# A gated cross-attention block on one core: exponentials transposed ahead of the next scores, first parts ahead of the rests, a bank taken out of turn, and jobs of other stages dealt anew

## The chip, the cores and the metric

The program runs on one core of a Trainium2 chip. The core has a TensorE (PE) with its own weight-load path (PEld), a VectorE (DVE), a ScalarE (ACT), a GpSimd (POOL) and a SyncE (SP), which only issues DMAs. Each engine works through its own instructions in the order in which they were written, and semaphores make one engine wait for another. The metric is the device time of one execution in microseconds; the kernel before takes 729.53 us, the median of 4 runs (728.73 to 730.4).

## The reference

`x` holds 8 sequences of 256 tokens by 512 numbers, that is 16 tiles of 128 tokens. Four blocks are added to it one after another:

```
x = x + tanh(g_xattn[0]) * conv_mixer(ctx, ctx, layernorm(x), ssm_kernel, D, head_dim 8)
x = x + tanh(g_ffn[0])   * bitlinear_ffn(layernorm(x), w1, w2, w3)          # 512 -> 1408 -> 512
x = x + tanh(g_xattn[1]) * masked_attention(layernorm(x), ctx, mask)        # 256 keys, no projections
x = x + tanh(g_ffn[1])   * one_bit_ffn(layernorm(x), w1, w2, w3)            # 512 -> 2048 -> 512
```

- The mixer multiplies the context with itself inside each of 32 heads (8 by 8 products), convolves each product along 512 places with the head's kernel, and contracts with the query.
- The first feed-forward network rounds activations to 8 bits per row and weights to -1, 0, 1.
- The attention takes softmax(x ctx^T / sqrt(512)) over unmasked keys and reads the context out with it.
- The second network rounds activations to 8 bits per group of 64, and takes the sign of its weights times their mean magnitude.

## The kernel before

All instructions of each engine are in an order written out by hand; a Python line that is called earlier stands earlier in the queue of its engine. Pools give out buffers in turn, and a buffer's next user waits for its last one.

**Stage 1, the mixer** (about 12 to 181 us of the profile), runs over 32 heads `h`. In each turn ACT copies the query and the context twice side by side (`q_twice`, `ctx_twice`, L307), POOL forms the pair products `kv` (L320, L326) and adds the halves of the earlier products (L388), TensorE runs 20 matmul records (L343) into one of three double banks of `ps_y`, ACT copies a few columns (`half_wrap`, L353), and DVE multiplies with the query (`half_products`, L365, L371, L378) and reduces (L393). A half of a head's matmuls may start when DVE has done the products that lay in its bank three halves earlier. Between these, a table of jobs deals out other work by turn and by slot of the turn: `job(h, "dve", f)` puts `f` behind DVE's products of turn `h`, `"act"` ahead of ACT's column copies, `"pool"` near the end and `"late"` at the very end of the turn. Jobs that matter here prepare stage 2: `first_stats` and `first_inverse` (DVE), `first_sqrt` (ACT) take the layernorm numbers of the first four tiles in pairs `g`; `first_by_act` takes those of tiles 4 to 7 on ACT by five instructions (L154 to L158); `front_norm`, `front_max`, `front_int`, `front_turn` normalise, find the row maximum, round and transpose (by DMA) a tile.

**Stage 2, the first network** (181 to 303 us), runs over the 16 tiles `t`. Three `up_block`s make two products each in banks of `ps_mm` (four banks; `pa`, `pb`, L852), ACT takes Silu of one (`sl`, L860), DVE multiplies (`hh`, L861); then the row maximum (L512), the rounding (L1000, L1018), a transposing DMA to `hqT`, and the product `down0` (L869) two turns later. `ps_o` and `ps_mm` lie where stage 1's `ps_y` was, and the first bank of `ps_mm` is given to a tile `passed` that is never used. `ln_finish` (L166 to L181) turns four tiles' variances into reciprocal roots, three DVE and fourteen POOL instructions.

**Stage 3, the attention** (303 to 380 us), again runs over the tiles. TensorE's order in turn `t` is: `scores(t)` (L938, 8 records), `e_transposed(t-1)` (`tre`, L959, 2 records), `x_transposed(t+2)` (`tr`, L927, 4 records), `readout(t-1)` (`po`, L967, 4 records). `masked` (DVE, L946 to L948) adds the mask and takes the maximum; `exponentials` (ACT, L953) follows; the transposed exponentials are copied out of PSUM by ACT to `eT` (L961), and the readout takes `eT`. ACT also normalises tile `t+3` (L195) and converts pieces of the last network's weights: `w1_signs(k)` issues the load of piece `k` into one of three buffers `w1st`, and its `make` takes the sign (L840) and, for the third matrix, also the sum of magnitudes (L842). `SIGNS[t]` says how many pieces are loaded in turn `t`; they are made in the next turn. Pieces 24 to 31 belong to the second matrix, 32 to 47 to the third.

**Stage 4, the last network** (372 to 728 us): a value is split into a first part `hi` and a rest `lo` (L1135, L1140), and each product runs over both with the same weights `w1q` (`up_products`, L1160; `down`, L1345).

The start issues some matmuls that nothing reads (`warm`, L664): 8, then two small ones, then 10.

Of the kernel before, what the change touches and what calls it, by code (L numbers as in the profile page):

```python
# [21 lines left out]
P = 128  # L22
# [20 lines left out]
def flamingo_gated_kernel(  # L43
# [159 lines left out]
    def load_table(func):  # L203

        nc.scalar.activation(junk1, ln_eps, func)
# [339 lines left out]
    def job(h, slot, f, *a):  # L545
        jobs.setdefault((h, slot), []).append((f, a))
# [71 lines left out]
    for k, h in enumerate(steps1):  # L618
        job(max(h - 2, steps1[k - 2] if k > 1 else 0), "late", load_w1a, k)
        job(h, "act2", abs_w1, k)  # L620
        if k % N1 == N1 - 1:
# [3 lines left out]
            job(h + 2, "dve", mean_w1, i)  # L625
    for g, h in enumerate((22, 25)):
        for k in range(2):
            job(h + k, "dve", first_stats, 2 * g + k)
        job(h + 1, "late", first_sqrt, g)
        job(h + 2, "dve", first_inverse, g)  # L630
    for k in range(2):
# [7 lines left out]

    for k, h in enumerate((24, 25, 28, 29)):  # L640
        job(h, "late", first_by_act, GRP + k)

# [18 lines left out]
    def warm(n):  # L661

        for _ in range(n):
            nc.tensor.matmul(pt[:, :P], ident, ident, start=True, stop=True)  # L664
# [6 lines left out]
    )  # L671
    warm(10)

# [135 lines left out]
    assert not jobs  # L809
    load_table(AF.Silu)  # L810

# [5 lines left out]

    ps_mm.tile([P, 512], F32, tag="mm", name="passed")

# [163 lines left out]
    for t in range(NT + 1):  # L983
        new = t + 2 < NT
        if t < NT:
            hh = p2.tile([P, FF0], F32, tag="hh", name="hh")
        if new:
            front_norm(t + 2)
# [7 lines left out]
        if t < NT:  # L996
            up_block(*x0[t], hh, 0)
        if 1 <= t:
            q = p1.tile([P, FF0], I8, tag="i8h", name="i8h")
            nc.scalar.activation(q, h_.pop(t - 1), AF.Copy, scale=sc)  # L1000
# [30 lines left out]
        if t > 2:  # L1031
            hqT, f3 = hq_.pop(t - 2)
            d_[t - 2] = (down0(hqT), f3)
        if t in FINISH:
            ln_finish(*FINISH[t])
# [17 lines left out]
        sums = []  # L1053
        if t == 0:
            clip_by_act(2, 3)
        if t == 3:
# [95 lines left out]
    def up_products(xT, f):  # L1152

        f0 = f * 512
        pa = ps_mm.tile([P, 512], F32, tag="mm", name="pa4")
        pb = ps_mm.tile([P, 512], F32, tag="mm", name="pb4")
        for i, pp in ((0, pa), (1, pb)):
            for c in range(NL):
                for k in range(2):
                    nc.tensor.matmul(  # L1160
                        pp,
                        xT[k][:, c, :],
                        w1q[i][:, c, f0 : f0 + 512],
                        start=(c == 0 and k == 0),
                        stop=(c == NL - 1 and k == 1),
                    )
        sl = px.tile([P, 512], F32, tag="sl", name="sl4")
        nc.scalar.activation(sl, pa, AF.Silu, scale=wmean1[:, 0:1])  # L1168
        return pb, sl
# [7 lines left out]

    SIGNS = [2, 2, 2, 2, 1, 2, 1, 1, 2, 1, 2, 1, 1, 1, 1]
    e_, r_ = {}, {}
    for t in range(NT + 2):  # L1180
        if t >= 2:
            residual(t - 2, *r_.pop(t - 2))
        if t < NT and t not in ps_:
            ps_[t] = scores(xT_.pop(t), keys[t // 2])
        if 1 <= t <= NT:
            e, den = e_.pop(t - 1)
            fac = small.tile([P, 1], F32, tag="fac", name="fac")
            nc.vector.reciprocal(fac, den)
            nc.vector.tensor_scalar(fac, fac, gates3[(t - 1) // 2], None, ALU.mult)
        if t < NT:  # L1190
            s_nmx = masked(ps_.pop(t), negs[t // 2])
        if t == NT:
            xn4, q, back = front(1)
            times(xn4, q, back)
            up_gate(hh[:, 0:512], *up_products(xT, 0))
        if 1 <= t <= NT:
            eT = e_transposed(e)

        if t == NT - 2:
# [7 lines left out]
        if t + 3 < NT:  # L1207
            xn_[t + 3] = normalised3(t + 3)
        for make in signs:
            make()  # L1210
        signs = []
        if t == NT:
# [36 lines left out]
        if t < len(SIGNS):  # L1249
            signs = [w1_signs(made + k) for k in range(SIGNS[t])]  # L1250
            made += SIGNS[t]
# [218 lines left out]
```

## Time and profile before

| what | value |
|---|---|
| median of 4 runs | 729.53 us (728.73 to 730.4) |
| the profiled execution | 730.04 us, of which the span is 728.2 us |
| TensorE busy | 713.8 us, 98% of the span, 3212 records |
| VectorE / ScalarE / GpSimd busy | 601.5 / 373.9 / 258.4 us |
| time on the chain that ended last, by engine | TensorE 87%, DVE 3%, ACT 2%, DMA 2% |
| stage 1 convolution matmuls (L343) | 640 records, 160.7 us |
| stage 4 products (L1160, L1345) | 1536 records of about 390 ns each |

The times are read like this: a TensorE record's start follows the start of the record before it by the time that the array needs, and its printed length is longer, since records overlap. So idle time of TensorE is found by comparing starts, not by adding lengths. "[0.95 <-DVE prod L378]" at the end of a row means that the engine stood idle for 0.95 us before that instruction and what ended it.

### The profile page before, as it was taken

The numbers are of one execution on the slowest core, as the hardware profiler recorded it, in microseconds if no ns is written. First come the engines' busy times: TensorE is split into PE (matmuls) and PEld (weight loads), VectorE is DVE, ScalarE is ACT, GpSimd is POOL, SyncE is SP. The second block draws the span as 40 slices with busy tenths as digits, with TensorE's granted clock in tenths as the row PEclk, the third lists the DMA queues.
The fourth block names the chain that finished last, engine by engine and source line by source line (L and its number), as shares of the span: only waits on it lengthen the run. The fifth ranks groups of instructions, "written<-read, shape, count | busy, mean of one in ns | idle before, by whom it ended". The sixth has DMA issues, their size and how long they took to land.

```text
span 728.2 us, 10153 instructions
## 1 busy us (share of the span) xinstructions
PE 713.8 (98%) x3212; PEld 531.9 (73%) x3212; DVE 601.5 (83%) x1224; ACT 373.9 (51%) x672; POOL 258.4 (35%) x363
## 2 busy tenths in 40 slices
PE   8999999998999999999999999999999999999997
PEld 6777777776554444566678788888888888888885
DVE  5799889998898887687867988988888988777965
ACT  5677787777778776767742322322212332212322
POOL 4888998989884535433300020000200002000000
PEclk9999999999999999999999999999999999999999
DMA  5865676821146567687604544645554544555443
GB/s 196 269 230 158 205 246 214 275 68 29 36 102 150 136 145 182 154 276 210 204 1 97 115 108 103 111 101 107 119 111 86 108 110 98 117 111 94 99 90 86
DMA packets 149970, 99.36 MB, mean 136 GB/s; under 512 B 83806, under 2 KB 127838, under 8 KB 149918
## 3 DMA queue, kind: packets, MB, share of 16 engines
q1 hardware_dynamic: 149608, 98.38, 52.4%
q0 software_dynamic: 256, 0.26, 0.5%
q8 instruction: 25, 0.41, 0.2%
q14 instruction: 27, 0.22, 0.1%
q10 hardware_dynamic: 54, 0.08, 0.1%
HBM read 75.58 MB, written 5.03 MB: 111 GB/s over the span
## 4 chain that ended last, share of the span: by engine, by line
PE 87%; DVE 3%; ACT 2%; DMA 2%; issue 1%; POOL 1%; SPq 0%; DVEq 0%; ACTq 0%
PE y L343 20%; PE po L1345 16%; PE pb L1160 15%; PE pa L1160 15%; PE po L967 4%; PE po L869 4%; PE pa L852 4%; PE pb L852 4%; PE ps L938 3%; DMA hqT<-qh 1%; PE tr_back L418 1%; DMA w1st<-in_L_w2t 1%; DVE am L512 1%; PE tr L410 1%; DMA sT<-d 1%
## 5 line engine op out<-in xcount | busy, mean ns | idle before, releaser
L343 PE MATMUL y<-kv,toep 128*128 128x288 f32 x640 | 160.7, 407 | 1.6 <-DVE rstd L128 0.8
L343 PEld LDWEIGHTS y<-kv,toep 128*128 128x128 f32 x640 | 119.3, 190 | 34.3 <-ACT y L353 2.1
L1168 ACT ACTIVATE sl<-pa,wmean 128x512 f32<-128x512 f32 x64 | 44.0, 688 | 187.6 <-PE pa L1160 187.6
L1160 PE MATMUL pa<-w,hi 128*128 128x512 f32 x256 | 100.6, 393 | 0.0
L1160 PE MATMUL pb<-w,hi 128*128 128x512 f32 x256 | 99.7, 390 | 0.5 <-DVE hh L1172 0.5
L1345 PE MATMUL po<-w,lo 128*128 128x512 f32 x256 | 99.9, 390 | 0.0
L1160 PE MATMUL pa<-w,lo 128*128 128x512 f32 x256 | 99.7, 389 | 0.0
L1345 PE MATMUL po<-w,hi 128*128 128x512 f32 x256 | 99.6, 389 | 0.0
L1160 PE MATMUL pb<-w,lo 128*128 128x512 f32 x256 | 99.6, 389 | 0.0
L175 POOL TENSOR_TENSOR nwt<-rstd 128x4 f32<-128x4 f32 x33 | 6.6, 199 | 240.9 <-DVE rstd L170 239.2
L320 POOL TENSOR_TENSOR kv<-cx 128x1024 f32<-128x1024 f32 x32 | 60.6, 1894 | 22.6 <-ACT cx L307 22.2
L852 PEld LDWEIGHTS <-xqT 128*128 128x128 bf16 x384 | 37.5, 98 | 39.9 <-issue 2.9
L388 POOL TENSOR_TENSOR prod<-prod 128x1024 f32<-128x1024 f32 x28 | 66.3, 2368 | 0.4 <-DVE prod L378 0.4
L1135 ACT CAST hi<-v 128x512 fp32r<-128x512 f32 x64 | 39.1, 622 | 48.4 <-DVE v L1335 48.4
L1172 DVE SCALAR_TENSOR_TENSOR hh<-pb,wmean,sl 128x512 f32<-128x512 f32 x64 | 47.7, 745 | 14.2 <-PE pb L1160 14.2
L1160 PEld LDWEIGHTS pb<-w,hi 128*128 128x128 f32 x256 | 48.1, 188 | 10.9 <-DVE hh L1172 1.0
L1345 PEld LDWEIGHTS po<-w,lo 128*128 128x128 f32 x256 | 48.1, 188 | 10.9 <-DVE lo L1140 1.0
L1160 PEld LDWEIGHTS pa<-w,hi 128*128 128x128 f32 x256 | 48.1, 188 | 10.4 <-issue 0.5
L1160 PEld LDWEIGHTS pa<-w,lo 128*128 128x128 f32 x256 | 48.1, 188 | 10.4 <-DVE lo L1140 0.2
L1160 PEld LDWEIGHTS pb<-w,lo 128*128 128x128 f32 x256 | 48.1, 188 | 10.0
L1345 PEld LDWEIGHTS po<-w,hi 128*128 128x128 f32 x256 | 48.1, 188 | 9.9
L365 DVE TENSOR_TENSOR prod<-y,qx 128x512 f32<-128x512 f32 x64 | 43.7, 683 | 9.3 <-ACT y L353 3.9
(160 smaller groups left out, 1345.3 us busy)
## 6 DMA issues: line engine op xcount, KB each, us to landing
sT<-d SPq DMA_DIRECT2D x64, 256.0 KB
toep<-ssm_skip SPq DMA_DIRECT2D x31, 256.0 KB
ch<-in_ctx_heads SPq DMA_DIRECT2D x32, 128.0 KB
w1a<-in_L_w1t SPq DMA_DIRECT2D x8, 512.0 KB
w1a<-in_L_w2t SPq DMA_DIRECT2D x8, 512.0 KB
w1st<-in_L_w1t SPq DMA_DIRECT2D x16, 256.0 KB
w1st<-in_L_w2t SPq DMA_DIRECT2D x16, 256.0 KB
cT<-in_ctx_t SPq DMA_DIRECT2D x8, 512.0 KB
```

The costliest lines, as they stand in the source:

```text
L320: nc.gpsimd.tensor_tensor(kv[:, :, 0 : ND * HD].rearrange("p a (i d) -> p a i d", d=ND), cx[:, :, 0:HD].unsqueeze(3).to_broadcast([P, NL * ...
L343: nc.tensor.matmul(y[:, k, :, W0 : W0 + NPAIR], toeps[h][:, d * P : (d + 1) * P], kvs[h][:, mi * B : (mi + 1) * B, :].rearrange("p b n -> ...
L365: nc.vector.tensor_tensor(prod[:, 0, r, :, :], yv[:, :, W0 : W0 + ND * HD].rearrange("p a (i d) -> p a i d", d=ND), view(q, [HX, n], [1, H ...
L388: nc.gpsimd.tensor_tensor(flat[0], flat[0], flat[1], ALU.add)
L852: nc.tensor.matmul(pp[:, :fw], xqT[:, c, :], w0q[i][:, c, f0 : f0 + fw], start=(c == 0), stop=(c == NL - 1),)
L869: nc.tensor.matmul(po, hqT[:, c, :], w0q[2][:, c, :], start=(c == 0), stop=(c == NF0 - 1))
L967: nc.tensor.matmul(po, eT[:, c, :], cN[:, c, :], start=(c == 0), stop=(c == S // P - 1))
L1135: nc.scalar.copy(hi, v)
L1160: nc.tensor.matmul(pp, xT[k][:, c, :], w1q[i][:, c, f0 : f0 + 512], start=(c == 0 and k == 0), stop=(c == NL - 1 and k == 1),)
L1168: nc.scalar.activation(sl, pa, AF.Silu, scale=wmean1[:, 0:1])
L1172: nc.vector.scalar_tensor_tensor(hh, pb, wmean1[:, 1:2], sl, op0=ALU.mult, op1=ALU.mult)
L1345: nc.tensor.matmul(po, hT[b][k][:, c, :], w1q[2][:, b * NL + c, :], start=(b == 0 and c == 0 and k == 0), stop=(b == NB - 1 and c == NL - ...
```

## The change

- In stage 1, `first_stats`, `first_sqrt` and `first_inverse` move to other turns: pair 0 from turns 22, 23, 23, 24 to 19, 21, 21, 23, pair 1 from 25, 26, 26, 27 to 23, 24, 24, 28. The last two `first_by_act` move from the ends of turns 28 and 29 into the `"act"` slot of turns 29 and 30.
- The second run of `warm` has 4 matmuls and not 10.
- The load of the Silu table is now brought about by an instruction that writes a column of `passed`, the first bank of `ps_mm`. With that, the first `pa` of stage 2 waits for the products of half-head (30, 1), the second `pa` for those of (31, 0), and the second `pb` for this instruction; before, the first `pa` waited for those of (31, 0).
- In stage 2's first turn, `front_norm(2)` (ACT) comes behind the first `up_block` and `ln_finish` (DVE, POOL) behind the third.
- In stage 3, turns 1 to 15 transpose the exponentials of the tile before (PE) and copy them out (ACT) ahead of `residual`, `scores` and `masked`. No pieces are made in turn 0, and the two left from stage 2 are made in turn 1 together with turn 0's one. `SIGNS` begins 1, 2, 2, 2, 2, 2 and not 2, 2, 2, 2, 1, 2.
- In stage 4's `up_products`, the loop over first part and rest is now outside that over the four column blocks: four matmuls with `hi`, then four with `lo`.

```diff
-    for g, h in enumerate((22, 25)):
-        for k in range(2):
-            job(h + k, "dve", first_stats, 2 * g + k)
-        job(h + 1, "late", first_sqrt, g)
-        job(h + 2, "dve", first_inverse, g)
+    for g, (h0, h1, h2) in enumerate(((19, 21, 23), (23, 24, 28))):
+        job(h0, "dve", first_stats, 2 * g)
+        job(h1, "dve", first_stats, 2 * g + 1)
+        job(h1, "late", first_sqrt, g)
+        job(h2, "dve", first_inverse, g)
...
-    for k, h in enumerate((24, 25, 28, 29)):
-        job(h, "late", first_by_act, GRP + k)
+    for k, at in enumerate(((24, "late"), (25, "late"), (29, "act"), (30, "act"))):
+        job(*at, first_by_act, GRP + k)
...
-    warm(10)
+    warm(4)
...
-    load_table(AF.Silu)
...
-    ps_mm.tile([P, 512], F32, tag="mm", name="passed")
+    passed = ps_mm.tile([P, 512], F32, tag="mm", name="passed")
+    nc.scalar.activation(passed[:, :1], ln_eps, AF.Silu)
...
-        if new:
+        if new and t > 0:
             front_norm(t + 2)
...
             up_block(*x0[t], hh, 0)
+        if t == 0:
+            front_norm(t + 2)
...
-        if t in FINISH:
+        if t in FINISH and t > 0:
             ln_finish(*FINISH[t])
...
         if t == 0:
+            ln_finish(*FINISH[t])
             clip_by_act(2, 3)
...
         for i, pp in ((0, pa), (1, pb)):
-            for c in range(NL):
-                for k in range(2):
+            for k in range(2):
+                for c in range(NL):
                     nc.tensor.matmul(
...
-    SIGNS = [2, 2, 2, 2, 1, 2, 1, 1, 2, 1, 2, 1, 1, 1, 1]
+    SIGNS = [1, 2, 2, 2, 2, 2, 1, 1, 2, 1, 2, 1, 1, 1, 1]
     e_, r_ = {}, {}
     for t in range(NT + 2):
+        if 1 <= t <= NT:
+            e, den = e_.pop(t - 1)
+        if 1 <= t < NT:
+            eT = e_transposed(e)
         if t >= 2:
             residual(t - 2, *r_.pop(t - 2))
         if t < NT and t not in ps_:
             ps_[t] = scores(xT_.pop(t), keys[t // 2])
         if 1 <= t <= NT:
-            e, den = e_.pop(t - 1)
             fac = small.tile([P, 1], F32, tag="fac", name="fac")
...
-        if 1 <= t <= NT:
+        if t == NT:
             eT = e_transposed(e)
-
...
-        for make in signs:
-            make()
-        signs = []
+        if t > 0:
+            for make in signs:
+                make()
+            signs = []
...
         if t < len(SIGNS):
-            signs = [w1_signs(made + k) for k in range(SIGNS[t])]
+            signs += [w1_signs(made + k) for k in range(SIGNS[t])]
             made += SIGNS[t]
```

## The prediction

> **What bounds the kernel now.** I read three views in this order: busy times and chain, the timeline of an attention turn, the waits. The profile page first:
>
> ```profile
> PE 713.8 (98%) x3212; PEld 531.9 (73%) x3212; DVE 601.5 (83%) x1224; ACT 373.9 (51%) x672; POOL 258.4 (35%) x363
> PE 87%; DVE 3%; ACT 2%; DMA 2%; issue 1%; POOL 1%; SPq 0%; DVEq 0%; ACTq 0%
> ```
>
> TensorE is busy 98% of the span and carries 87% of the chain that ended last. The change removes only six warm-up matmuls, at the start; so elsewhere it can gain only what TensorE loses between starts. I compared each TensorE start with the one before and the usual spacing of that kind, and added up what was over: about 4.9 us in the first 20 us, 4.6 in 140 to 193 (the end of the mixer and the first turn of the network), 1.0 at 292.7, 6.5 in the attention, 0.9 at 401.5 to 402.5, and in 420 to 700 only 0.06 per 20 us. The last network, over 40% of the time, is full.
>
> An attention turn, by the timeline of 326 to 340 us (start, length, engine, line; the last number in brackets is idle time and what ended it):
>
> ```profile
> 330.27 0.38 PE L959 MATMUL tre<-ident,s 128*128 128x128 f32 x2
> 330.49 0.60 PE L927 MATMUL tr<-ident,xn 128*128 128x128 f32 x4
> 330.69 0.37 ACT L961 COPY eT<-tre 128x256 f32<-128x256 f32 x1 [1.37 <-PE tre L959]
> 331.11 0.30 PEld L967 LDWEIGHTS po<-cN,eT 128*128 128x128 f32 x2 [0.26 <-ACT eT L961]
> 331.11 1.98 PE L967 MATMUL po<-cN,eT 128*128 128x512 f32 x4
> 331.13 0.51 ACT L953 ACTIVATE s<-s,nmx 128x256 f32<-128x256 f32 x1
> 332.34 0.61 ACT L840 ACTIVATE w<-w1st 128x512 fp32r<-128x512 f32 x1
> 332.93 1.89 PE L938 MATMUL ps<-cT,xT 128*128 128x256 f32 x8
> ...
> 334.80 0.19 ACT L842 ACTIVATION_READ_ACCUMULATOR w1st<-w1st 128x1 f32 x1
> 334.86 0.42 DVE L946 CUSTOM_DVE_ANT_0 s<-ps,neg 128x256 f32<-128x256 f32 x1 [0.66 <-PE ps L938]
> 335.08 0.37 ACT L961 COPY eT<-tre 128x256 f32<-128x256 f32 x1
> ```
>
> See that a turn of TensorE is 4.39 us (tre 330.27 to 334.66), and that the four `tr` records (0.44) are all that covers the copy `eT`; the readout comes 0.19 after its place, and its first weights are not ahead: 1.82 from the readout's start to the next scores, where a readout without the wait takes 1.71 (367.35 to 369.06). So a turn loses 0.19 + 0.105 = 0.29. See also that ACT, from 331.13 to 334.99, makes an exponential, a normalisation and two pieces of weights that each need a sign and a magnitude sum.
>
> **The change, part by part.** The base is the profiled execution, 730.04 us (span 728.2 and 1.8 around it), 0.5 above the median of 729.53.
>
> *Attention order, gain.* With `tre` ahead of the scores, copy and `eT` have the eight score records (1.73) and `tr` (0.44) as cover, against 0.37 of copy. The turns of tiles 4 to 12 have nine waits of 0.29: -2.65. Tile 3 has 0.35: -0.35. The second readout of the stage waits 1.42 at 311.91, because `eT` stands on ACT behind two signs that wait for loads:
>
> ```profile
> 311.95 0.74 DVE L222 SCALAR_TENSOR_TENSOR xs<-po,fac,xs 128x512 f32<-128x512 f32 x1
> 312.50 0.63 ACT L840 ACTIVATE w<-w1st 128x512 fp32r<-128x512 f32 x1 [1.62 <-DMA w1st<-in_L_w2t]
> 313.03 0.35 ACT L961 COPY eT<-tre 128x256 f32<-128x256 f32 x1
> 313.44 1.12 PE L967 MATMUL po<-cN,eT 128*128 128x512 f32 x2 [1.26 <-ACT eT L961]
> ```
>
> The new order puts `eT` ahead of the signs, and these start a turn later. The readout then starts at about 312.0 and not 313.5, but the next `tre` now follows directly and has its own chain: masked scores at 312.92 (DVE's own order holds them there), exponentials at 313.63 to 314.14; TensorE would be free at 313.74. So 1.5 - 0.45, and with that turn's 0.35 the stage is about 1.4 earlier by tile 2. Together -4.4.
>
> *Attention order, price.* `tre(t)` now needs the exponentials before the next scores. From the end of the scores to the masked ones is 0.20, to the exponentials 0.86, to their end 1.37 plus issue; behind them lie `tr` and readout, 2.15. About 0.7 is left, so TensorE does not wait, if ACT comes at once. But `eT` and the exponentials now have ACT's longest turns between them: ACT needs 0.70 for the exponentials and their sum, 0.71 to the next free place for `xn`, 2.63 from 332.34 to the end of the second magnitude sum at 334.99, and 0.37 for `eT`: 4.41 in all, more than a turn of 4.10. Where `eT` must come 3.68 after the exponentials' start less 0.27 of copy and semaphore, it comes 0.73 late, and 0.17 more in a turn directly behind such a one (its exponentials shift too). By `SIGNS`, pieces from 32 on carry magnitude sums; the turns with two of them are tiles 5, 6, 9 and 11, and tile 4 has one (0.1). 0.73 x 3 + 0.17 + 0.1 = 2.46. I take it whole; it is 0 if the loss is hidden by DVE or by a load that comes later anyway, and it doubles if the late `tre` makes the scores' masks late too, on DVE (83% busy). The number of pieces and loads is 22 before and after; SP's queue has the loads behind those of `cT` and `cN` as before, a turn later for the first pieces, of which ACT has three in turn 1. The waits of ACT for `w1st` are 5.2 us in four places; the first two of these (1.47 and 1.62) move behind `eT`. Sum of the attention: **-1.9**, bounds -4.4 and +0.5.
>
> *End of the mixer.* `first_stats(3)` and `first_sqrt(1)` come earlier: ACT's wait of 1.31 at 161.72 goes, by which column copies and so TensorE were late at 159.66 (0.56). In place of it ACT waits at turn 24 for DVE's statistics (about 150.8 against ACT free at 149.9), 0.95; behind that instruction stand `first_by_act`, the copies of query and context, then POOL's pairs. By hand, the pairs of turn 28 come 1 us later (161.4 against 160.45), and by turn 30 TensorE is 0.4 earlier (the two late `first_by_act` are only moved, 1.7 of ACT each). At the passage into the network:
>
> ```profile
> 178.63 1.86 PE L343 MATMUL y<-kv,toep 128*128 128x288 f32 x7
> 181.45 1.02 PE L852 MATMUL pa<-w,xqT 128*128 128x512 bf16 x4 [0.95 <-DVE prod L378]
> ```
>
> This 0.95 goes, since the first product now takes a bank that was free earlier. But who comes next? ACT loads the Silu table (1.28 from 181.18) and normalises (0.80 from 182.58) before the first Silu at 183.29; moved behind, the normalisation frees 0.7, and the first `hh` would be at 183.4 to 183.7 against 183.99. The banks after that are released at the pace of DVE and ACT. `ln_finish` moves too: its DVE part once took 1.40 beside a POOL instruction (others 0.17), and moved to the turn's end it delays the maximum `am`, for which I get 189.1 against 188.98. So TensorE waits later what it waited at 181.45. I take **-0.2** for both, with bounds -1.8 (what a whole passage would be worth) and +0.9 (turn 24's wait, kept to the end).
>
> *Start.* Six `warm` matmuls less. They run at 0.11 each up to 8 us; the first transposes wait for `xnp` (ACT, 7.80, first weights at 8.01), the next for POOL (10.93). So **0**: the cover is that chain. What they might be worth is that the clock is up. The profile shows a granted clock of 1.00 throughout; but starts are 0.21 apart from 1.46 to 5.2 us and 0.11 from 5.79 on. The 1.62 of idle time before 10.93 did not bring the longer spacing back. [...]
>
> *Last network.* Both orders have the same 1536 records, weights and moving data. The rest `lo` is in time: the only such row is the 0.24 of the weights at 371.73, and it lies under the last readout matmul (four by 0.43 from 369.90 or later). Spacing is 0.2266 with either kind. **0**, bounds -0.8 (two such starts of 0.41 over spacing, 371.32 and 380.83, taken as true) and +1.
>
> Sum: 730.04 - 1.9 - 0.2 = 727.9 in such an execution, less 0.5: **727.4 us** for the median.
>
> **The rivals.** *Whole gain*: ACT catches up within slack, the magnitude turns cost nothing: -4.4, and -0.8 at the passage: 724.3. For it: ACT is only 51% busy, and one turn's lag may be taken by slack of the next. Against: 4.41 in a turn of 4.10 is arithmetic.
>
> *Hidden anyway*: readouts are no longer late, but three pieces in turn 1, their loads and the longer ACT turns return nearly all: -0.5, so 729.0. For it: "ACT w L840" waits 5.2 us for loads and DMA queues are busy (0.79 in 303 to 318). Against: the nine regular waits have no load in them.
>
> *Clock lost, slower*: with six warm matmuls fewer the array is back at the longer spacing when the transposes begin. Work of 8.1 to 17.0 us is
>
> ```profile
> 8.10:17.00 8.90, 7.11 (x46) 5.46 (x45) 7.00 (x23) 6.53 (x13) 4.03 (x4) 1.00 0.50 166
> ```
>
> that is 7.11 us of TensorE, which at twice the spacing is 7.1 more, less 1.8 of idle cover at 9.0 to 10.9: +5.3. With my -2.1 it is +3.2, or 732.7. It decides if it costs more than 3.6 us. Against: six matmuls are a short pause beside the 1.62 that did no harm.
>
> **How the numbers follow.** Forecast 0.50, whole gain 0.22, hidden 0.20, clock lost 0.08. A measurement can tell 0.2%, 1.46 us: faster is below 728.07, slower above 730.99. Forecast: between its bounds mostly faster, 0.34 faster, 0.12 same, 0.04 slower. Whole gain: 0.22 faster. Hidden: 0.07 faster, 0.11 same, 0.02 slower. Clock: 0.02 same, 0.06 slower. Sum 0.63, 0.25, 0.12. The range goes from -6 (the attention whole with a passage at nearly its bound: 723.8) to +1.1 (730.6; both upper bounds, 0.5 and 0.9, less what is unlikely to meet). The forecast's own range is 725.9 to 729.0.
>
> **What would show it.** Right: no idle time before `po` L967 in tiles 3 to 5, a turn of 4.10 there, and about 0.7 before `po` in tiles 5, 6, 9 and 11 ended by `eT`; `masked` waits as before. The first `pa` starts near 180.5, with new idle time before the following products. Starts 0.11 apart at 8 to 17 us; spacing in the last network unchanged. Wrong: turns of 4.10 throughout (whole gain); 0.21 between transposes at 8 us (clock); waits for `w1st` or exponentials of 1 us or more in the attention (hidden); pairs in stage 1 more than 1 us late after turn 28.

## The result and the profile after

The changed kernel takes 731.08 us, the median of 53 executions, against 730.04 us for the kernel before (78 executions on the same chips): 1.0019 times the time, 95% interval 1.0012 to 1.0025, so 0.9 to 1.8 us longer. The forecast was 727.4. The fastest quarter of its executions ends at 730.04 (before: 729.01), the slowest quarter begins at 732.40 (before: 730.87): it is later throughout, and most at the slow end. Its profiled execution took 730.46 us with a span of 728.4, 0.2 more than before's.

The page of the changed kernel, busy engines and the chain that ended last:

```profile
PE 711.2 (98%) x3200; PEld 529.9 (73%) x3200; DVE 600.2 (82%) x1224; ACT 372.5 (51%) x672; POOL 258.3 (35%) x363
PE 77%; POOL 6%; DVE 4%; ACT 4%; issue 4%; DMA 2%; SPq 0%; DVEq 0%; POOLq 0%; ACTq 0%
```

The six matmuls that are gone are 12 records (3212 to 3200). TensorE's part of the chain fell from 87% to 77%, and POOL's rose from 1% to 6%: from about 112 to 160 us the chain now runs largely through POOL's pair products and additions. The timeline of the changed kernel in the mixer, TensorE's turns 21 to 24 (start, length, engine, line; in brackets the idle time before and what ended it):

```profile
125.42 0.62 ACT L307 COPY cx<-ch 128x512 f32<-128x512 f32 x1 [1.42 <-DMA ch<-in_ctx_heads]
...
134.10 0.68 DVE L118 BATCH_NORM_STATS2 st<-xs 128x6 f32<-128x512 f32 x1
134.82 0.18 DVE L119 BATCH_NORM_AGGREGATE mv<-st 128x2 f32<-128x6 f32 x1
134.92 0.66 DVE L365 TENSOR_TENSOR prod<-y,qx 128x512 f32<-128x512 f32 x1
135.03 0.29 ACT L123 ACTIVATE std<-mv,ln_eps 128x2 f32<-128x2 f32 x1 [0.94 <-DVE mv L119]
135.24 0.60 ACT L307 COPY qx<-qT 128x512 f32<-128x512 f32 x1
135.74 0.61 ACT L307 COPY cx<-ch 128x512 f32<-128x512 f32 x1
...
136.18 2.27 DVE L395 TENSOR_REDUCE qT<-prod 128x256 f32<-128x2048 f32 x1
...
136.44 1.89 POOL L320 TENSOR_TENSOR kv<-cx 128x1024 f32<-128x1024 f32 x1 [0.75 <-ACT cx L307]
...
138.58 0.69 DVE L365 TENSOR_TENSOR prod<-y,qx 128x512 f32<-128x512 f32 x1
...
140.10 2.18 PE L343 MATMUL y<-kv,toep 128*128 128x288 f32 x8 [0.66 <-DVE prod L378]
```

and the same products of the kernel before:

```profile
133.11 0.67 DVE L365 TENSOR_TENSOR prod<-y,qx 128x512 f32<-128x512 f32 x1
...
134.40 2.27 DVE L395 TENSOR_REDUCE qT<-prod 128x256 f32<-128x2048 f32 x1
...
136.80 0.69 DVE L365 TENSOR_TENSOR prod<-y,qx 128x512 f32<-128x512 f32 x1
```

At 140.10 TensorE waits for a bank that DVE's products release (those from 138.58 on; before, from 136.80 on), and from 130.80 to there DVE has no idle time. So the products are late by what stands ahead of them on DVE. About 0.9 us of the lateness came in at 125.42, where ACT's copy waits 1.42 us for a load (0.55 in the profile of the kernel before, but 1.27 to 1.65 in ten of the eleven others with the old turns). The rest is `first_stats` of the second tile (L118, L119, 0.86 us), which now precedes the products of 134.92. The profile of e17, a kernel below that has the old turns and the same 1.42, separates the two: its turn 24 takes 5.43 us, that of the changed kernel 6.19, that of the kernel before 5.29. So 0.76 belongs to the statistics. The square root of the first pair, now at the end of turn 21, waits 0.94 us for them on ACT, with the copies of query and context behind it; that wait is not what held DVE here.

The second square root (151.92, a wait of 1.06 us for DVE) does hold the copies behind it, and POOL stands idle for 3.65 us until it makes the next pairs at 155.25. Turn 25 begins 1.00 us later than before, turn 29 2.09; turn 31 is 1.13 late. At the passage:

```profile
181.46 1.03 PE L852 MATMUL pa<-w,xqT 128*128 128x512 bf16 x4
182.27 0.31 ACT L353 COPY y<-y 128x192 f32<-128x192 f32 x1
...
184.00 0.67 ACT L860 ACTIVATE sl<-pa,f 128x512 f32<-128x512 f32 x1
...
188.60 1.26 DVE L166 TENSOR_SCALAR nwv<-mv 128x4 f32<-128x4 f32 x1
...
190.47 1.60 DVE L512 TENSOR_REDUCE am<-hh 128x1 f32<-128x1408 f32 x1
...
193.21 0.81 PE L852 MATMUL pb<-w,xqT 128*128 128x384 bf16 x4 [1.91 <-DVE hh L861]
```

The first `pa` has no wait any more. But counted from the start of turn 31 (176.61), the row maximum `am` comes at 13.86 us (before 13.50) and this last `pb` at 16.60 (before 16.25). What were two waits for the kernel before (0.95 and 0.63) is one wait of 1.91.

In the attention the new order does what it should in most turns. The rows around the exception:

```profile
330.61 0.61 ACT L840 ACTIVATE w<-w1st 128x512 fp32r<-128x512 f32 x1
331.25 0.63 ACT L842 ACTIVATE w1st<-w1st 128x512 f32<-128x512 f32 x1
331.88 0.35 ACT L961 COPY eT<-tre 128x256 f32<-128x256 f32 x1
332.22 0.51 ACT L953 ACTIVATE s<-s,nmx 128x256 f32<-128x256 f32 x1
...
332.29 1.98 PE L967 MATMUL po<-cN,eT 128*128 128x512 f32 x4 [0.32 <-ACT eT L961]
...
336.49 1.88 PE L967 MATMUL po<-cN,eT 128*128 128x512 f32 x4
```

Where ACT has made two pieces with magnitude sums, `eT` is late (332.29, and again at 349.28 and 358.07: 0.48 late and 0.10 for the weights each time); the readout at 336.49 waits for nothing, and turns without the wait are 4.10 us.

### The profile page after: what moved, and what is told of

It reads as the page before. It is cut to its first block, busy times and chain, and to the rows that moved or that the text cites. A ratio compares the mean times of both kernels' runs of the same rounds, so it can differ in the third digit from the quotient of the medians.

```text
span 728.4 us, 10125 instructions
## 1 busy us (share of the span) xinstructions
PE 711.2 (98%) x3200; PEld 529.9 (73%) x3200; DVE 600.2 (82%) x1224; ACT 372.5 (51%) x672; POOL 258.3 (35%) x363
## 4 chain that ended last, share of the span: by engine, by line
PE 77%; POOL 6%; DVE 4%; ACT 4%; issue 4%; DMA 2%; SPq 0%; DVEq 0%; POOLq 0%; ACTq 0%
PE po L1354 16%; PE pb L1164 15%; PE pa L1164 15%; PE y L343 13%; PE po L869 4%; PE pa L852 4%; PE pb L852 4%; PE po L967 3%; POOL prod L388 2%; PE ps L938 2%; POOL kv L320 1%; DMA hqT<-qh 1%; DMA w1st<-in_L_w2t 1%; POOL w L477 1%; ACT w L840 1%
## 5 line engine op out<-in xcount | busy, mean ns | idle before, releaser
L1164 PE MATMUL pa<-w,hi 128*128 128x512 f32 x256 | 69.5, 393 | 0.0
L1164 PE MATMUL pb<-w,hi 128*128 128x512 f32 x256 | 68.6, 390 | 0.4 <-DVE hh L1176 0.4
L1164 PE MATMUL pa<-w,lo 128*128 128x512 f32 x256 | 68.5, 389 | 0.0
L1164 PE MATMUL pb<-w,lo 128*128 128x512 f32 x256 | 68.4, 389 | 0.0
L1164 PEld LDWEIGHTS pb<-w,hi 128*128 128x128 f32 x256 | 48.0, 188 | 10.8 <-DVE hh L1176 0.8
```

Source lines behind the costliest of these rows:

```text
L1164: nc.tensor.matmul(pp, xT[k][:, c, :], w1q[i][:, c, f0 : f0 + 512], start=(c == 0 and k == 0), stop=(c == NL - 1 and k == 1),)
```

## The experiments

Each kernel has 12 executions (e15 and e16: 11) against 23 to 35 of the kernel before on the same chip. "Low" counts the executions whose mean granted TensorE clock is below 0.9985; the kernel before has 37 such among 163 in these comparisons (23%), with a median of 731.8 us against 730.6 for its others, the changed kernel 21 among 54, with 732.5 against 730.2.

| kernel | median us | before us | ratio, 95% interval | low |
|---|---|---|---|---|
| e1 loop order undone | 733.00 | 730.85 | 1.0030, 1.0012 to 1.0048 | 9 |
| e2 attention alone | 730.06 | 730.85 | 0.9993, 0.9979 to 1.0007 | 5 |
| e3 mixer's end and passage alone | 732.71 | 730.85 | 1.0029, 1.0015 to 1.0043 | 6 |
| e4 loop order alone | 731.08 | 730.85 | 1.0003, 0.9993 to 1.0014 | 4 |
| e5 statistics' turns alone | 731.01 | 730.74 | 1.0007, 0.9997 to 1.0018 | 2 |
| e6 two first_by_act alone | 730.41 | 730.74 | 1.0004, 0.9993 to 1.0014 | 3 |
| e7 bank passed alone | 730.09 | 730.74 | 0.9992, 0.9979 to 1.0004 | 3 |
| e8 network's first turn alone | 730.81 | 730.74 | 1.0006, 0.9994 to 1.0017 | 4 |
| e9 changed, warm(10) | 731.88 | 730.76 | 1.0011, 0.9999 to 1.0023 | 6 |
| e10 before, warm(4) | 730.83 | 730.76 | 1.0008, 0.9993 to 1.0024 | 3 |
| e11 changed, start filled | 732.71 | 730.76 | 1.0017, 1.0005 to 1.0030 | 8 |
| e12 before, start filled | 731.10 | 730.76 | 0.9998, 0.9984 to 1.0013 | 0 |
| e13 attention and passed | 730.14 | 730.85 | 0.9991, 0.9981 to 1.0001 | 3 |
| e14 changed, start filled in the transpose's bank | 731.14 | 730.85 | 1.0004, 0.9994 to 1.0015 | 3 |
| e15 as e14, passage filled | 732.23 | 730.85 | 1.0019, 1.0007 to 1.0030 | 4 |
| e16 attention, old SIGNS | 730.99 | 730.85 | 0.9999, 0.9988 to 1.0011 | 4 |
| e17 e13, start filled | 729.69 | 730.94 | 0.9989, 0.9976 to 1.0001 | 0 |
| e18 changed, old jobs | 732.55 | 730.94 | 1.0013, 0.9995 to 1.0030 | 8 |

Most single effects are near what 12 executions can tell. So the profiles are read by segments as well, between starts of TensorE: from turn 1 to turn 31 of the mixer; from there to the attention's first `tre`, without the one wait for `hqT` near 295 us (it is 0.49 to 2.10 over the profiles, with no relation to the kernel); from `tre` to the last scores. Medians over the profiles:

| segment | with the part | without it | difference |
|---|---|---|---|
| mixer, by the statistics' new turns | 157.4 (8 profiles, 157.03 to 157.75) | 156.7 (12, 156.44 to 156.98) | +0.65 |
| to the attention, by the passage's parts together | 127.5 (6, 127.45 to 127.79) | 127.3 (12, 127.14 to 127.56) | +0.2 |
| attention, by the new order with new SIGNS | 60.2 (10, 59.45 to 61.68) | 60.9 (9, 60.62 to 61.85) | -0.7 |
| from the last scores to the end, by the loop order | 362.5 | 362.5 | 0 |

(e15 and e18 are left out of the second row: the one has matmuls added there, the other loses its clock there.)

**Four parts of the change, each taken out or put in alone (e1 to e4).** e1 undoes the loop order in the changed kernel, and e4 makes it in the kernel before:

```diff
-            for k in range(2):
-                for c in range(NL):
+            for c in range(NL):
+                for k in range(2):
```

> The changed kernel with one part undone: the last network's products run again over first part and rest inside the loop over the column blocks. Theory A (the loop is worth nothing, since the rest is in time and the records are the same): span within 0.4 us of the changed kernel's 728.4 and a median within 0.5 us of its 731.1. Rival B (the new order, which changes the weights at every record, lets the granted clock fall more often: the changed kernel's executions at a granted clock of 0.993 to 0.998 took 731.1 to 734.4 us, those at 0.999 and 1.000 mostly 729.1 to 730.7): median 1 us lower than the changed kernel's, and few executions below 0.999.

> The kernel before with the last network's loop order alone. Theory A: within 0.4 us of before, spacing of the products unchanged at 0.227 us. Rival B (granted clock): about 1 us slower than before, with more executions below a granted clock of 0.999.

Rival B fell: e1 has more low executions, not fewer, and e4 is no different from the kernel before. Theory A's sizes for e1 were missed: the median (733.0) in an experiment with 9 low executions of 12, the span (729.2) in a profile at the full clock, whose attention has three readouts 0.6 to 0.8 us late behind signs with late loads. The segment behind the attention shows no difference. The loop is worth nothing that these runs resolve.

e2 is the hunk of stage 3 and nothing else (the moved `e_transposed`, `SIGNS`, `t > 0` and `+=`).

> The kernel before with the attention's part alone (transposed exponentials ahead of the scores, and the new SIGNS with no pieces made in turn 0). Theory A (the attention gains what the two traces show between its first transposed exponentials and its last scores, 1.6 us, and the mixer's end and the passage lose it): faster than before by 1.2 to 2.2 us, with the readout late only where two pieces with magnitude sums are made. Rival (the attention gained only because it began 1.95 us later and its loads had landed by then): within 0.6 us of before, with new waits for w1st.

It gained 0.5 us by the ratio, and its interval holds zero: less than Theory A, and within the rival's number, though not for its reason, since no new wait for `w1st` shows. The three late readouts are there, 0.48 each. What is smaller is the gain, and another profile says why. The second readout of e3, which has the old order, by its timeline:

```profile
313.48 0.36 ACT L961 COPY eT<-tre 128x256 f32<-128x256 f32 x1
...
313.89 1.98 PE L967 MATMUL po<-cN,eT 128*128 128x512 f32 x4 [0.18 <-ACT eT L961]
```

This is the readout that waited 1.42 us at 311.91 in the profile on which the forecast was built. In the eight other profiles with the old order it comes 0.19 to 0.34 behind its place: that one execution had a long wait that is not usual (its loads for `w1st` landed at 310.25 and 312.50), and the attention's usual length is 60.9, not 61.85.

e3 is the hunks of stage 1, the Silu table, `front_norm` and `ln_finish`.

> The kernel before with the parts around the mixer's end alone: the new turns of first_stats, first_sqrt, first_inverse and first_by_act, the Silu load by a column of passed, front_norm and ln_finish moved in the first turn of the first network. Theory A: slower than before by 1.3 to 2.2 us; turn 25 begins about 0.9 us late, and the first transposed exponentials of the attention come about 1.9 us late. Rival (it is the loop or the warm-up that costs): within 0.5 us of before.

Theory A held by the ratio, 2.1 us slower (1.1 to 3.1), though half of its executions are low and its profile, with a span 0.6 longer than before's, is not.

**The parts of e3 by themselves (e5 to e8).** e5 is the first hunk of the change (`first_stats`, `first_sqrt`, `first_inverse`), e6 the second (`first_by_act`), e7 `passed` in place of `load_table(AF.Silu)`, e8 `front_norm` and `ln_finish`:

```diff
-    for g, h in enumerate((22, 25)):
...
+    for g, (h0, h1, h2) in enumerate(((19, 21, 23), (23, 24, 28))):
```

> The kernel before with the new turns of first_stats, first_sqrt and first_inverse alone. Theory A (ACT's square root now waits for the statistics at the ends of turns 21 and 24, 0.94 and 1.06 us in the changed kernel, and the copies of query and context stand behind it): turn 25 begins 0.7 to 0.9 us late against turn 24, turn 28 another 0.4; the one old wait of 1.31 us in turn 26 is gone; first product of the network 0.3 to 1 us late, time 0 to +1.2 us. Rival (the waits are covered, what costs lies at the passage): turns as before, time within 0.4 us.

The turns came as late as Theory A said: turn 25 is 1.14 later against turn 24 (a little over the 0.9 expected), turn 28 another 0.46, turn 29 0.64, of which 1.0 is regained by turn 31. The segment of the mixer is 157.75, the longest of all. That the square roots cause all of it is not shown: in turn 24 TensorE waits 0.90 us for DVE's products, as in the changed kernel, and ahead of these stand the statistics themselves. The time, +0.5 us (-0.2 to +1.3), agrees but does not show it alone.

```diff
-    for k, h in enumerate((24, 25, 28, 29)):
-        job(h, "late", first_by_act, GRP + k)
+    for k, at in enumerate(((24, "late"), (25, "late"), (29, "act"), (30, "act"))):
+        job(*at, first_by_act, GRP + k)
```

> The kernel before with the last two first_by_act alone moved, from the ends of turns 28 and 29 ahead of ACT's column copies of turns 29 and 30. Theory A (1.7 us of ACT now stand ahead of the last column copies and of the Silu table): the first Silu and hh of the network come 0.7 to 1.4 us late, the first row maximum with them, time +0.4 to +1.2 us. Rival (ACT has the slack there): first Silu as before at 183.3, time within 0.4 us.

The rival held: the first Silu comes 7.82 us after turn 31 begins, before 7.81.

```diff
-    load_table(AF.Silu)
...
-    ps_mm.tile([P, 512], F32, tag="mm", name="passed")
+    passed = ps_mm.tile([P, 512], F32, tag="mm", name="passed")
+    nc.scalar.activation(passed[:, :1], ln_eps, AF.Silu)
```

> The kernel before with the Silu table loaded by writing a column of the first bank, passed, and nothing else. Theory A (the wait of 0.95 us ahead of the first product only moves behind it, since the first hh is set by ACT and DVE): first product 0.9 us earlier, second row maximum and the attention's start within 0.3 us of before, time within 0.5 us of before. The three kernels with this part had 2.06 to 2.10 us around their spans and the others 1.76 to 1.85; if that belongs to this part, 0.3 us of time is lost outside the span here. Rival (the bank is a real gain): attention's start 0.7 us earlier or more.

Theory A held: counted from turn 31 the first `pa` is 1.1 earlier, a new wait of 0.67 for `hh` follows, and the segment to the attention is 127.14, as before. The 0.3 us around the span are not here (1.78).

```diff
-        if new:
+        if new and t > 0:
             front_norm(t + 2)
...
-        if t in FINISH:
+        if t in FINISH and t > 0:
             ln_finish(*FINISH[t])
```

> The kernel before with front_norm(2) behind the first up_block and ln_finish behind the third in the network's first turn, and nothing else. Theory A (ACT reaches the first Silu 0.7 us sooner, DVE finishes the third hh before the slow statistics instruction of 1.2 to 1.4 us, which then delays the row maximum as before): first hh 0.3 us earlier or more, row maximum of the first hh within 0.3 us of before's 188.98, time within 0.4 us. Rival (the slow instruction and the later normalisation come on top): row maximum 0.7 us late or more, time +0.5 us or more.

Theory A held: from turn 31 the first Silu 7.11 (before 7.81), the first `hh` 8.14 (8.51), `am` 13.54 (13.50).

**The start (e9 to e12).** Two of the first profiles had a mean granted clock below 1: it fell to 0.50 to 0.67 between 12 and 16 us, at an idle stretch of 1.99 us in e5 and 2.79 us in e8, while TensorE waited for POOL's `xnp`. So theory C: what the median shows is lost there. e9 has the changed kernel with `warm(10)`, e10 the kernel before with `warm(4)`; e11 (changed) and e12 (before) add

```diff
     pair_turn(0, 1)
+    fill = [ps_y.tile([P, 2, B, YB], F32, tag="y", name="fill") for _ in range(3)]
+    for _ in range(8):
+        nc.tensor.matmul(
+            fill[0][:, 0, :, W0 : W0 + P // B], ident, ident, start=True, stop=True
+        )
```

> The changed kernel with the second warm-up back at 10 matmuls. Theory C (what the median shows is the granted clock at the start: in two profiles it fell to 0.50 to 0.67 between 12 and 16 us after an idle stretch of 1.99 and 2.79 us, the executions with a mean granted clock below 0.9985 are about 2.2 us longer, and the changed kernel has 21 of 54 of them against 14 of 70 of the kernel before): fewer such executions, about 3 of 12, and a median near 730.3 us. Rival A (the mixer's end costs what the median shows): median unchanged near 731.1.

> The kernel before with the second warm-up cut to 4 matmuls, and nothing else. Theory C: more executions below 0.9985, 5 of 12 or more, and a median 0.5 to 1.5 us above before. Rival (a wait for the first transposes hides the six matmuls and nothing else changes): as before, 2 or 3 of 12, median within 0.4 us.

> The changed kernel with 8 more matmuls that nothing reads between the second and the third of the first transposes, where TensorE stands idle for 1.6 us or longer. Theory C: no execution below 0.9985 or one at most, and a median of 729.6 to 730.4 us, below the changed kernel's. Rival (the clock falls elsewhere, or these executions are long for another reason): the share stays at 4 or 5 of 12 and the median near 731.

> The kernel before with the same 8 matmuls. Theory C: no execution below 0.9985 or one at most, median 0.2 to 0.6 us below before; beside the changed kernel with them it shows what the rest of the change is worth at an undisturbed clock, by the executions so far between -0.5 and +0.3 us. Rival A: the changed kernel with them is 1 us or more slower than this one.

Theory C held for e12 alone: with the stretch filled, none of 12 executions is low, but the median did not fall with it. e9 and e11 kept their low executions, and neither tells where. e9's own profile loses the clock at the start (from 12.27 us, in an idle stretch of 2.67). e11 has another passage than the changed kernel: in its profile the first product of the network waits for the instruction that writes `passed`, where the changed kernel has no wait:

```profile
183.95 1.02 PE L857 MATMUL pa<-w,xqT 128*128 128x512 bf16 x3 [2.50 <-ACT passed L823]
```

In e10 the median is as before, yet three executions have a clock of 0.992 to 0.995, and the mean is 731.5 against 730.9. Its profile shows a third kind of start: records of `warm` and of the transposes stay 0.21 us apart, those of the first products 0.48, until 17.7 us, and turn 1 begins at 22.76 (before 19.04). In the profiles with `warm(10)` the spacing first becomes 0.11 between 4.4 and 6.2 us or between 9.5 and 10.8, and never later.

**The passage (e13 to e16).** The question was where the changed kernel loses its clock: theory D said at the passage, in the wait of 1.91 us. e14 and e15 fill the second idle stretch of the start, into the next transpose's own bank, and e15 adds 16 matmuls ahead of that `pb`; e13 joins e2 and e7; e16 is e2 with the old `SIGNS` and their making in turn 0:

```diff
+    early = ps_tr.tile([P, NL, P], F32, tag="tr", name="tr")
+    for _ in range(8):
+        nc.tensor.matmul(early[:, 0, :], ident, ident, start=True, stop=True)
...
-    pair_turn(1, 1)
+    trs[pairs[1][1]] = early
+    for c in range(NL):
+        nc.tensor.transpose(early[:, c, :], ps_[1][0][1][:, c * P : (c + 1) * P], ident)
...
+            if fill and i == 1:
+                spare = [ps_o.tile([P, L], F32, tag="o", name="po") for _ in range(2)]
+                for _ in range(fill):
+                    nc.tensor.matmul(spare[0][:, :P], ident, ident, start=True, stop=True)
```

> The kernel before with the attention's part and the bank passed, the two parts that were not slower alone. Theory D (these gain 0.3 to 0.8 us each by the executions so far, and leave the passage without a stretch of idle time that costs the clock): faster than before by 0.5 to 1.5 us, 0 or 1 of 12 executions at a granted clock of 0.995 or less. Rival (the gains were noise of the start): within 0.4 us of before.

> The changed kernel with 8 matmuls that nothing reads ahead of the third of the first transposes, written into that transpose's own bank, so that no bank is taken out of turn. Theory D (the changed kernel loses the clock at the passage): still 3 to 7 of 12 executions at 0.995 or less, 2 to 3 us longer than the others; if its profile is one of them, half clock between 191 and 200 us. Rival C (the clock is lost at the start alone): none, median near 730.

> As the kernel before this, with 16 more matmuls that nothing reads in the network's second turn, between the last pa and pb, where TensorE waits 1.9 us for hh. Theory D: 0 or 1 of 12 executions at 0.995 or less, median 729.5 to 730.5 us. Rival: as many low executions as without them.

> The kernel before with the transposed exponentials ahead of the scores, but SIGNS and the making of pieces as before. Theory A (ACT's turns with magnitude sums delay eT by 0.5 to 0.8 us each): readouts late in the turns behind two pieces of the third matrix, those of tiles 8 and 10 at least, and no gain or loss against e2 beyond 0.8 us. Rival (SIGNS is what makes the order pay): 1 us slower than e2, with new waits in the first turns.

e14 and e15 do not bear theory D out: one and two executions at 0.995 or less. e15 is inconclusive besides, since a matmul is two records, and its 16 held TensorE for 3.4 us where 1.9 were to be filled (counted from the first `pa`, that `pb` came 1.5 us later than in the changed kernel). Neither fills the first idle stretch of the start, ahead of the first transposes (0.92 us in e14's profile), so the 7 low executions among their 23 may still come from there. e13 is 0.7 us faster by the ratio, with zero just inside the interval; its one low profile lost the clock from 11.2 to 18.0 us, at the start, in an idle stretch of 2.25. In e16 readouts are 0.48 late near 337, 350 and 359 us, behind magnitude sums, and 0.7 and 0.4 late near 315 and 324; it is 0.4 us above e2, within Theory A's bound, with some of the early waits that the rival named.

**Two last kernels (e17, e18).** e17 is e13 with the start filled as in e14. e18 puts the old two job tables back into the changed kernel, so that e5 and e6 are undone.

> The kernel before with the attention's part, the bank passed and 8 matmuls that nothing reads ahead of the third of the first transposes, in that transpose's own bank; the warm-up stays at 10. By the segments: attention 0.6 us shorter, mixer and network as before, 1.8 us around the span, and fewer executions with a lower granted clock: 0.6 to 1.4 us faster than before. Rival (what the first parts gain is taken back by the start): within 0.4 us of before.

> The changed kernel with the old turns of first_stats, first_sqrt, first_inverse and first_by_act. Theory A (these jobs carry the loss): mixer from turn 1 to turn 31 back to 156.4 to 157.0 us from 157.5, 127.2 us instead of 127.5 from there to the attention without the wait for hqT, median 0.7 to 1.5 us below the changed kernel's and not above before's. Rival (the loss is the start's, with its four warm-up matmuls): median as the changed kernel's, 1 us above before.

e17 is the fastest of all: no low execution, and 0.8 us faster than before (interval -1.8 to +0.1). It beats the changed kernel, whose interval lies wholly above its own; against the kernel before it is likely, not shown. e18 brought the mixer back (156.79) as Theory A said, but not the median: 8 of 12 executions are low, and four others took 729.0 to 731.3. Its profile happens to be the longest of them, at a mean clock of 0.992, and shows where. Windows of e18 (window, its length, PE, PEld, DVE, ACT and POOL busy, granted clock, DMA share, GB/s):

```profile
4.00:8.00 4.00, 2.55 (x18) 2.13 (x17) 2.96 (x11) 1.73 (x4) 2.31 (x2) 0.98 0.98 351
8.00:12.00 4.00, 2.92 (x13) 2.53 (x14) 3.83 (x14) 3.05 (x6) 0.77 (x2) 0.50 0.53 195
12.00:16.00 4.00, 4.00 (x17) 3.21 (x16) 2.00 (x10) 3.00 (x6) 2.54 (x2) 0.66 0.59 197
...
192.00:196.00 4.00, 2.02 (x12) 1.09 (x11) 3.43 (x8) 2.73 (x4) 2.93 (x14) 0.95 0.17 33
196.00:200.00 4.00, 4.00 (x15) 2.02 (x14) 2.99 (x6) 3.07 (x6) 3.73 (x6) 0.62 0.49 92
```

and its timeline at the two places:

```profile
8.05 1.97 PE L410 MATMUL tr<-ident,xnp 128*128 128x128 f32 x8 [1.03 <-ACT xnp L195]
...
193.99 0.81 PE L852 MATMUL pb<-w,xqT 128*128 128x384 bf16 x4 [1.85 <-DVE hh L861]
...
195.37 1.66 PE L852 MATMUL pa<-w,xqT 128*128 128x512 bf16 x4
```

The clock falls first at 7.88 us (a mean of 0.98 over 4 to 8 us), in the idle stretch of 1.03 us that the six warm-up matmuls used to fill; eight transposes take 1.97 us and not 1.19. It falls again behind the 1.85 us wait for `hh`: four `pa` records take 1.66 us where four took 1.03. The segment from turn 31 to the attention is 1.5 us longer than in the other profiles (128.78 against 127.3). In e17's profile, where the spacing becomes 0.11 only at 9.55 us, no fall follows:

```profile
8.00:12.00 4.00, 3.76 (x27) 3.52 (x26) 3.83 (x13) 2.42 (x6) 0.95 (x2) 1.00 0.57 213
12.00:16.00 4.00, 4.00 (x31) 3.63 (x31) 1.70 (x7) 2.81 (x6) 1.18 (x2) 1.00 0.59 197
```

So both places are shown, in one execution. Twelve executions of one kernel cannot tell the shares apart; all of them together tell more. By an estimate, a mean clock of 0.995 over a span of 730 us stands for some 7 us at half the clock; e13's profile, with a mean of 0.995, has 6.8 us of it. The kernel before has 1 such among 163, and the eight kernels with ten warm-up matmuls and without the new mixer's end and passage together (e2, e4 to e8, e13, e16) have 2 among 95. With four warm-up matmuls and an unfilled start there are 26 among 90 (the changed kernel 13 of 54, e1 5, e10 3, e18 5 of 12 each); e10 differs from the kernel before in the warm-up alone (3 of 12 against 1 of 163). So the cut warm-up costs the clock in a share of the executions. With ten warm-up matmuls and the new mixer's end and passage there are 4 among 24 (e3, e9). That is more than without them, but which of their parts does it is open. And the two kernels with ten warm-up matmuls and the second stretch filled (e12, e17) have no low execution among 24, where 5 or 6 would be usual.

## Why the prediction was wrong

**Attention, gain, forecast -4.4: the mechanism was right, a third of the size was not there.** The nine regular waits of 0.29 went. The term of 1.4 for the first two tiles rested on one wait of 1.42 us in one execution; in the eight other profiles of the old order that readout is 0.19 to 0.34 late. The median over executions to which the sum was applied holds no such wait, so it could not be gained. The price of 0.45 that the term was netted against did come: in all ten profiles of the new order with the new `SIGNS`, TensorE waits 0.54 us for the exponentials ahead of the third `tre`.

**Attention, price, forecast 2.46: nearly right.** Three readouts are late by 0.59, 1.77 together; the 0.17 and the 0.1 that were added did not show. In seven of the ten profiles one or more readouts of the first turns are late as well, mostly by 0.2 to 0.8, behind signs whose loads are late. Forecast for the whole -1.9; the segments show about -0.7, and -1.6 against the one profile.

**End of the mixer, forecast -0.2 with the passage: the step that failed.** I followed the second pair's square root on ACT (turn 24; 0.95 forecast, 1.06 measured) and put the earlier statistics of the first pair at nothing. They stand on DVE, which has no idle time there, ahead of products that release TensorE's banks, and cost 0.76 in turn 24. The catching up was overrated too: turn 30, forecast 0.4 early, is 1.54 late. The mixer is 0.65 longer in the segments.

**Passage.** That the wait only moves behind the first product was right, as was `am` (forecast 189.1; 190.47 less the 1.13 of the late turn 31 is 189.3). What I did not cost is that waits of 0.95 and 0.63 are now one of 1.91. The clock fell behind such a wait in e18's profile (1.85), not in the changed kernel's (1.91) or e14's (1.90).

**Start, forecast 0: the second step that failed, wrong in its size and its reasoning.** A warm-up matmul is two records of 0.11 us (six matmuls are 12 records fewer), so the six are 1.3 us of work, not 0.66, and the stretch that they leave open was not costed. I went by one stretch of 1.62 us in one execution, behind which the longer spacing did not come back. The runs show the clock falling in a stretch of 1.03 us (e18), in or just behind five of 1.85 to 2.79 (e5, e8, e9, e13, e16), and not behind five of 1.62 to 1.67 (before, after, e1, e3, e7). No run shows the 0 for executions at large: with the warm-up alone cut (e10), 3 of 12 executions have a clock of 0.995 or less, and 1 of 163 of the kernel before. In the changed kernel's own profile the start cost nothing, which is why only other executions show it. The rival "clock lost" named the place (8 to 17 us) and had a chance of 0.08; it happens in a share of executions. The changed kernel's 13 executions at 0.995 or less have a median of 732.9 us, its 33 at the full clock 730.2.

**Last network, forecast 0:** right, as far as these runs resolve.

**The sum.** By segments: +0.65 mixer, +0.2 to the attention, -0.7 attention, and +0.3 that lies around the span (2.08 us in the changed kernel's executions against 1.77), together about +0.5. For the clock there is an estimate from the executions: 21 low ones of 54, 2.3 us longer than the others, put 0.9 us on the changed kernel's mean, and 37 of 163, 1.2 us longer, put 0.3 on that of the kernel before. The difference of 0.6 and the 0.5 of the segments make 1.1, beside 1.04 between the medians and 1.35 between the means (731.34 against 729.99). How the 0.6 divides between start and passage is open. So is the cause of the 0.3 around the span: none of e5 to e8 has it whole (1.76, 1.89, 1.78, 1.84), nor has e18 (1.87); e3 has (2.07), and so has e17 (2.01), which lacks most of these parts. And 0.5 of the distance between 727.4 and 731.08 lies in the base: four executions of the kernel before had a median of 729.53, 78 have 730.04.

## What to carry to other kernels

A wait that one profile shows is a sample: before a gain is built on it, look for it in the profile of another execution, and count a chance wait for a load as noise. When a job is moved to an earlier turn on an engine that works in order, ask of every one of its instructions whether its input is ready there and what stands behind it. Here a square root of 0.3 us waited 1.06 for its input and held copies and pairs behind it, and 0.86 us of statistics on an engine without idle time held the products behind them for about 0.8. Waits that are gathered into one, and fillers taken out of an idle stretch, have a price that the profiled execution need not show: at two such places TensorE's clock fell to half in e18's profile (idle for 1.03 and 1.85 us) and stayed at 1.00 in the changed kernel's (0.86 and 1.91).

## What the runs showed of the hardware

- The same program starts in several ways. Matmul records of 128 columns go from 0.21 to 0.11 us apart between 4.4 and 6.3 us, between 9.5 and 10.8 us, or (e10) at about 17.7 us. The 20 records of `warm(10)` take 2.50 us in the profiles of the kernel before, e3, e5, e7 and e8, and 4.38 to 4.64 in those of e2, e4 and e6. Turn 1 of the mixer begins at 19.04 us in the profile of the kernel before and at 22.76 in e10's.
- The profile's granted clock reads 1.00 while records are still 0.21 us apart at the start (until 4.4 us at the earliest, in e10 until 17.7). From 12 to 16 us TensorE works on 14 records in 4.00 us of busy time in e10 at a clock of 1.00, 13 in 4.00 in e13 at 0.50, and 22 in 3.83 in the kernel before at 1.00. So the spacing has to be read as well.
- A fall takes the clock to half (windows of 0.50 in e5, e13 and e18). By the means of the windows it lasts 3.40 to 3.44 us (e5, e8, e9, e16, e18 from 195.61) or 6.8 to 6.9 us (e13: 0.90, 0.50 and 0.75 over 8 to 20 us; e18 from 7.88: 0.98, 0.50 and 0.66 over 4 to 16 us).
- The length of an idle stretch does not decide alone: the clock fell in one of 1.03 us (e18) and not behind five of 1.62 to 1.67. Nor does the busy time just before: in the 3.41 us up to its second fall e18's TensorE is busy for 1.49 us, and the clock falls; in the 3.41 us up to 193.40 in the changed kernel it is busy for 1.50, and the clock stays. What else decides is not shown.
